# Layer 3's x on its way through DRAM: written in pieces of 128 bytes, read in runs of 512

## The chip, the cores and the metric

One Trainium2 chip, one of its cores. The metric is the device time of one launch of the whole kernel in microseconds (us). The kernel before takes 2758.63 us (median of three runs, 2754.33 to 2764.74).

## The reference

32 graphs of 512 nodes with 256 features, float32. Each graph goes through four layers, and after each its input is added and the sum is normalised over the features (layernorm):

```python
x = _layernorm(x + _L0_gnn_ref(x, adj, ...))        # relu(((1+eps) x + adj @ x) @ W1 + b1) @ W2 + b2
x = _layernorm(x + _L1_gnn_ref(x, adj, ...))        # attention of 4 heads over the edges, adj > 0.5
x = _layernorm(x + _L2_gnn_ref(x, adj, ...))        # attention of 8 heads, scores + log(adj)
x = _layernorm(x + _L3_gnn_ref(x, nodemask, adj, W))
```

The change is in layer 3, whose body is

```python
intermediate = jnp.einsum('bsh,hd->bsd', matrix, W)
similarities = jnp.einsum('bsd,btd->bst', intermediate, matrix) * adj
attn = softmax(where(mask, similarities, NEG_INF))
output = jnp.einsum('bst,bth->bsh', attn, matrix)
```

`matrix` is layer 3's x, 512 x 256. Both products that make the similarities need it with the features on the partitions; the last product and the residual need it with the nodes there.

## The kernel before

**Graphs and steps.** `graph(g)` describes the work of one graph as some 340 named steps, each with an engine, the steps it comes after and the buffers it takes. The graphs overlap: while one is in its layer 3, others are in their layers 0 to 2. The order in which all steps are issued is fixed by a text, `ORDER` (L40), which names for each place the next step. `Plan.run` (L180) reads it; an engine's queue gets its steps in that order. The due times that `Plan.run` adds up from the steps' written costs decide only which free slot of a kind a step takes (`room[kind].sort()`): `p` are the eight PSUM banks, `C` twelve SBUF tiles of about 4 KB per partition.

**Queues.** Plain DMAs are issued by SP, in order, and each waits in SP's queue for what it needs: adjacency (`la`, L806), x (`lx`, L818), layer 1's row factors to DRAM and back (`Rs`, `xs`, `Rl`, `hsb`, L1030 to L1054), the turn of x3 (`xw`, `xl`, L695 and L708) and the output (L1581). POOL issues accumulating copies from SBUF to SBUF, which add up layer 2's exponentials (L1311 and L1364), and the additions of biases to x (L610). Both kinds run on the same 16 DMA engines; the profile calls POOL's queue q0 and SP's q1.

**Layer 3's x.** The layernorm after layer 2 ends with four ScalarE steps `r30` to `r33` (L669), one for each chunk `c` of 128 nodes (`NC` = 4), which write the tile `x3`, [128 nodes, chunk, 256 + 1]. `x3` then has to be turned. The first two graphs and the last three do it on TensorE (`features_first`, L1214). The other 27, g = 2 to 28, call `turned(3, ...)` (L690):

- `xw3i`: one DMA writes all of `x3` to a DRAM tile, 1 KB a piece, after all four r steps;
- `xl30i` to `xl33i`: four DMAs read it back, block `a` of 32 features to the partitions 32a to 32a + 31, 32 values (128 bytes) a piece, into the tile `xL3`;
- `xe30`, `xe31`: two VectorE transposes of 32 x 32 blocks (L727) finish it to `xT3`, [128 features, half d, 512 nodes].

TensorE's steps `i0` and `i1` (iT_ps, L1504, issued by the helper at L327 or L331) are the first to read `xT3`. Behind the reads in SP's queue stand the adjacency loads of a later graph, then the output of the graph before and its x load.

Of the kernel before, what the change touches and what calls it, by code (L numbers as in the profile page):

```python
# [34 lines left out]
def row_bcast(ap, n):  # L35
# [2 lines left out]


ORDER = (  # L40
    'c-rk;*^=bA4Fo}ux~uw{@%D}<?En8tBNL#idcEV=h<$Q|)H78&cp-6+Dx@SLCAZiUY;jy-Po=2(Kg9|4bIQx=--7b0qlKcZttiWH'
    ')UVi3wM1o+(N!sO?!@kSboLOnRjaZznpU2Y$`ZAfigFx>7Bf_=cD7N9##YpPD_$7~C|;ijj(UEXt@>3xHy;76N3rVlOPui!^;)B1'
    'Ze~6<@4HqL?@k{BpjaHe4@7HgrzkZB5`)A)G;N7_%hThlvR`h%*6Krqs$-zO7j<HsYzpl{fE;>AQ!w0m*00uTE2l8Ejf-A4WNBW2'
    '4MJq#X=SuP5JH6P#V`c+U=X@h%2q=WQG{DGQ3DOr?6X2uJYkwxL1k7$g_Vt?mKP{STpw^dE>;>3pc5T!q^Ja=mN0cfntHDR6-}+u'
    'nAw>=j45i>kgBHehK2<CjV1-9U<=_7rvXvZ8qx+z1{47&mBZEmQM3)%hf9v}c)M=zYHS5n6Q(Fnd<EK~4WKa&-#CIwtMEFK7{TzX'
    'p3qbXlF&YFUbSH)=?-kNp&5Ewbe=<S%;9PD$dqkZcJ2{<3sX+_hDA^m<M{mmmU5a0J8Z25=0@P9VJi?by7t06RU56#iy5^PaRg;h'
    'GeisdYJgaVh$S>b^Rn|)sQh6(3}7(?$T2Kf#z<w1Q#sPg0Og(pQ>8j62%3Od8l5dHDV6+i$d+EAh<`A9wm6hRkpe&jO64G2EtP(m'
    '8wZM^hA*bYmNYelfl3SEfZ3RL=!KflI2=QV)Au8+0o1~8|MI?JI_#{mE5x-C)lzpxZ*3INOQj;!LqWQviyxIEmN7<I3E^4@;u>x2'
    'Apms=TZo7c_=f?`5N~X1_Ap<AUHEbHCdE#WT{zcZ4b8!=>OdFB16mA+P1B7c=qW8PK*+wrXd)`){F0y0Tn)<-j8dL-BaX8vBk?)X'
    'CwqScyl9Mr8G&B{CkxwpY9Q=Y($P*)O&Fu9o)Muw1+a6@ezs%I5*6@1$`2J}Oy_jY*q&pz)MR#_A^xcaD<kwjnn~xvF|R63B(@BA'  # L50
    'Et*Dv$TKo#K&%ah{umasoc;>gazXn`XrGrp7ql0&S3tO+y`a6Iy<+VJ?FH=x?FH=x?FH?%Lb$B<g7$*;3J90gUeI39UeNxZLp!kj'
    'HMGp+Cb&%9NVcJW6WqT5ZK5}zwXfLzDYW*C?K3b5?Z_CX=p)}0=x1&X*{&ya?a@kkK>J5zllPHXb9|M|f%@1@42GGYR^S(TJ3vFS'
    'gm8~3GbG1kWYM%_ww6WfnK&K?nMT$$D;PgB&zZx+2NL|k%zlaT7;5IPp=eS9*mDpO+y=6PNDx{b8F>lorRJHjEX;~psI!h_xIL1f'
    'gQ8)CLn6bCTw$U0F{_xMG$v6a4=p2A3pR*>J;Nk6c_oE=HT<A*uLOmlW^2r;m(xrNE%x-SikvO`X+fSa=44x<m}$*OWoPDnWV4xO'
    'rXsXiQ=Fp=8oUK*k>jt7JCAH<&;o)H!*0BKWwJha0>vJw?MUtNvjHm6u#@6_fn*`T<D?c<ij^a@;05SOABY`46+lJ?`jKNDJ3#>o'
    'PKBPFof`6!fiw&k))n-L<dk4|O53*6w>?bAA2<{aQh2q7hf6SSf-@seA>d?-aOlBG0HdM~Z8AWC6VQTt60wdH9VY6NlH-#_8<Ip^'
    'Am;<(P<^ct`zG)Y39VQQEjrTL+8{QyWTk*okz6E1Y{%LQSwO1^q&=Vm!9?rB2K7PQ3By8L4Ky4wLO}RoqCROCtq{<Y?qosAAR7!#'
    'wV2~X2UF%G1u5h6X-;x-r0O6nJZnbU7e$$zWFc?{nkHw)P8wE5^FT2e4uhBi{)1^N5mGdQEj<k^H8Rx7@K4Mo3S-U?fMK-MHd+cV'
    '0UwKiLAf=(_hIV1lA<P$WE4V#X~_VAbC*yeSa=L1G&CD?bV&|PP@956!Hr6$PeC~~nMKe>b_Tl0=?|t4buqq?l43Pt6y2*?ix@fh'
    'UKwUi?uhD;ffOnwQ6ktTUnW%yMbeGgIs*?md58~SuW(wSl8WUuGF=$qp2Ic2O0iUXFpzZUi@GP%NFO{Zx)zNo)<_z@NLh8nuMymz'  # L60
    'uEh*$BTxs551F5tWlt*#D>(`2=}S*cks!u>xsdbKFm<cJ71L0J=`)+kNV1DL?qs!CdD2H!J^3!DcQa5Eu0c1-s^mW9e3=;VVoV!='
    '`AdbgB28-GSi?OQEa&3o!E3TX9IJu%SoTGe^e;PEI-&T{^yu%Y_3?f7KPZ0BOQWykoLHXyA<F+^8~5(=^70~^TP9p7*|s|Zn)O*~'
    '@8ZrORF?0z`rE&HndhYceOAP=36slUrg_mH|Nen?dhat?wI-W4b^}?k%Cz~J*CNLuNp(D;twV0xA$3O(srYgLUdt{<2Gazls@Ya!'
    'vW1Mx!d1so%H}hPY#Ro`722|FvhJ_bzAww$y1z&;A>H#_ggN$SHYMfdwk*s1rjxX7*-P1dh|{rcL8xOG*j&728jMsfLH%kYfyydp'
    ')mZHYO_|MC&W5q$AIA~vWrucO?+&*^l6NTQ>ePPrzAQgcwEN-a=(<z)*|cl>&GkKdG@Yi-MiomgF5O&nb8MJiK_}ya4Ae0nS}ZFt'
    'FP+P`bJ^qyVo$z5&s}ZjI&-PLF+@#PkJ>qOTUU<p_WgUEFpGTKNG!!1KFNgU=G)|ooF>-+{`JWRR2s47^yU*b_9pvLxo~t1%v@b^'
    '{n3H}yK%A>TD(Wmvbg43=j>o_Z*N|`LxqlsnWHg7Fi?U8En>AN6PlW^xh(&5$aT^=S$vJ>g8}X>4kPw~c!AkPpZYvQVO?HQCz2#$'
    'u6k|XcO1Vm-mZ+Mj$t=DjwR&m(5AcfauZvyJ8t9-xA$rFzY36e!-nOe*Pco{?Gs(jK(o8<=t8~_C|v4cwc3IN9H4$m-rIbBVzy=g'
    '2mZmfZSE3SpZS6d8lIO79<Hp`K?s#L^nf)0mfV0mjM!FL*Y)PQSV5|Voh&Nv-fwp;AXH2atHWgR3*dqE4DX|2+qn9yk{s{V!Sb!F'
    ';_+Z!mQuI2NSR?%Q&yTnt{HbS7LkrX)_t$jw`n0+Uu>!#tUO{JsF1|w!~a|dO_s3lnFgL-K*b4%io?a~&95#uU~D%~V_oHRk`U*H'  # L70
    'avjmgg^o2gZd2S*`ebofVI6S;=;2+Gyd6&^+$+4$73CU{@B9&>!z>ZJaK8gd=MKuJx|_MuK2(B=84nV0sFVuUO5GP2iA(CrpCUXT'
    'htllOoCOH(0t5_ee2{<%PLRSK&ENf8`y@D@9#uTJdNZ5WwJzTCBKPlJ`gViv-``d49+Tad%iRY7QE{Vuw{}buZiv3?#`{p=ZMnL4'
    'nnzF#-YXwwU|?_ym~PXwo6+MuSSzAIU-=LO@6d&ebW9<LU_n)-1;TYabOASSy3e?iS-gn_igllGjN(337!Lz}cu{e?Yz{D%hP)SR'
    '?m`|H_*@0b-AbV2H5;d`gZ08l;)xBfyU`=#gBI>GWP3QEcBBjgq(7dvB0;3~X~buw`tc#+&J;Hxkk@N;rKaFBh(bT$b+>P~+wJY`'
    '<6eSY??L9Zn#Tr}m)=*d;2p<0VWQvPxon3MV@h#k{P4}AY2SPj<ZVj)h(QZ@&tK^|H^-2DCeiP6JW0{sq^<V!Bfie_QrpU(m2e-;'
    'Cq&%sSHgfPQR3$isxD$y87m6TsT%kHyva4P(@V@UK{ggSpUSCYVEn<uBT@;RF$Fvx*@<7AQiyO4+`Am{^PV4nljOjEb9<pG@HPLy'
    '-Nk<+D;KoCgqFz41?>gx6%a0HFK91luULCQdqI0adqI0adqI1x5H72|puM2I0>Wjr7ql0&7qtK9(DpA>i2n)g6S#mEp9^wQe-GTh'
    '0Ik>;Xv<e@{}ftz#`XzXTExUR&Zri7Y$vvoL|+BC@{H~iy!H(37i7;jL-A!jkLH84z}M)M;+Xzp168gvE$st)Asa%G+5<17%O3hf'
    '%S%~jauXYk!Nl?Y{deThe)BH*TC4gbNqblfa{H~y{mzu#3ymgT=*Bd?%oYNi$@d}wN)wP$!2bP^$krWYyyfa0rEK@Xztp5E3#hpX'
    '6o?K%q>BtTSTuf;>D+u7QYD`_Xvg3>v~{qBnL`8#HEs4J*h?@e08+e_4xAEVy6+JYHqubHBI|hbkOa@6%rDs9nNGL&U>oXjl(eMa'  # L80
    'eTv-tug;>&0=5ei#4U)=Ose1K*=7YZ0K=bYEH2rq(rLf27Law*^8#z|GD=%poBPC3Pe=swZB=1hw<^ccigsOkDIc9Lc$<ptYcY~F'
    'KuTUIC|_}8i{R)ETO;&+DNMHGMQ%*ZN-~#PyJZ^P5gOV>#<)<gk4FR|NzQj4(R7&Dr8<Kz4!R&x<rK1h_}`n<R}hSE#WA~)uzvSH'
    '2YlBXPV9~#e2Bn%ESvWZlAP#DmLJT4<i|2B75p4H*ZqEP%>julv&fNl{Gkps^4PB{2fnVff_)ialavc+cam24_9<9r$IHCdW!uO;'
    '0Oi9S0;Hy1U7sFs$gzb(gRN25btP%rCM%$xfb1Y`3ZfGg5(I^&GQ58T&%Via-vC#zp4=|hSJjyu6mR%AmSd5!%p)M9m+)NV*f*xt'
    '%c_!3I#kX(jGEH=gcom-D-}T{JdXjvzOb*7RK_<k+IVlIkWE8^+RvY)1_15PPY>>U-L}e5-TLZ-nA>FG=ZusxO+L(Cl*AzLF_Kv5'
    'k^R>CQJKt73ZKLi7<^`c4^R{hmXE?Qx3U&!ZY}woNLhmOF^l7HxIItW+5(GPmgduTBSRAtgind{TzW0tx~pyuhD&V>Fz5&LDh$k>'
    '!-Aq3!JI_n7TzPl*1>T32T(vNnl<<gGpVcR{5SgrGPGQBVi%|3c1xFDdRZsBm?)`y;WeOu)tFwve~1W29u&BDV9UCZHkik%3$FB+'
    '7gUf<Q92aq1^Ys_G1(Wve+JbSd>}Bpx_0o>R!7=BppkfMKjE&+E5!V#n^f!hdO|*>BQ;);sBm6Cmun-56#zIIyzHWOpP=142nB-P'
    'yo0!+ZG9=OC@(RinEL-|_Fy}$n6{>%+aSg*HoM(fom-no@z621y88HTOH#hwL){)o0G08!$__5&H=ifo`fKesyS;go_RWKcuOnu#'
    '(Aqk=*MK6{z<?*AjqgVkkRQR8fn*a2quqm&#}gT=7kT5fccT&bMZbEx?LLz2=6c)Q;|bHg3@;jSbMrH6UG!Yyb;OEkt}ZYpKOnkp'  # L90
    'n<FvLQ_NyhFb!iO^C-55W%=OJjy!B{TZ1>8kM@*!FC%%~Twl1vMnYRIRtjl!2l;sC(xP}1>cSVFvUZso$Wq<{`DA3)c^qqYKB*ed'
    'RB#@ZF;SgQu^J<aoNJ@=9kgSg4{Lm_^w<{i`Pi}B-h__gO@8qb+3-gB4`D>{SO'
)


# [122 lines left out]
def fast_path(  # L218
# [363 lines left out]
    def graph(g):  # L582
# [106 lines left out]

        def turned(n, more, src):  # L690

            @step(f"xw{n}i", "sp", 0.45, row(f"r{n}", NC))
            def _():
                t[f"xd{n}"] = dram.tile([P, NC, D], F32, tag=f"x{n}_dram", name=f"x{n}_dram_{g}")
                nc.sync.dma_start(t[f"xd{n}"], t[src][:, :, :D])  # L695

            transfer(f"xw{n}", 1.5, (f"xw{n}i",), land=6.0)

            for a in range(4):

                @step(
                    f"xl{n}{a}i", "sp", 0.66, (f"xl{n}{a-1}i",) if a else (f"xw{n}",),
                    take=() if a else (f"C=xL{n}/{2 if n == 1 else 1}",) + more,
                )
                def _(a=a):
                    if a == 0:
                        t[f"xL{n}"] = mid(f"xL{n}", [P, NC * DC, P], f"xL{n}")
                    nc.sync.dma_start(  # L708
                        t[f"xL{n}"][32 * a : 32 * a + 32].rearrange("j k (e i) -> j k e i", i=32),
                        bass.AP(  # L710
                            t[f"xd{n}"].tensor, t[f"xd{n}"].offset + 32 * a,
                            [[NC * D, 32], [P, NC * DC], [32 * NC * D, 4], [1, 32]],
                        ),
                    )

                transfer(f"xl{n}{a}", 1.0, (f"xl{n}{a}i",), land=6.0)

            for d in range(DC):

# [4 lines left out]
                def _(d=d):  # L724
                    if d == 0:
                        t[f"xT{n}"] = mid(f"xT{n}", [P, DC, N], f"xT{n}")
                    nc.vector.transpose(  # L727
                        t[f"xT{n}"][:, d, :].rearrange("p (c f) -> p c f", c=NC),
                        t[f"xL{n}"].rearrange("p (c d) f -> p d c f", d=DC)[:, d],
                    )  # L730

            plan.free(f"xL{n}", row(f"xe{n}", DC))
# [1349 lines left out]
```

## Time and profile before

| | |
|---|---|
| median of three runs | 2758.63 us |
| the profiled execution, its own time | 2757.91 us |
| its span, first to last instruction | 2756.2 us |
| PE / DVE / ACT / POOL busy | 98% / 78% / 62% / 17% |
| DMA engines: q0 (POOL) / q1 (SP) | 53.4% / 24.4% of 16 engines |
| writes of x3 to DRAM | 27 of 512 KB |
| reads back | 108 of 128 KB |
| mean granted TensorE clock | 0.992 |

Times are microseconds from the first instruction. PE is TensorE's matmuls, PEld its weight loads, DVE VectorE, ACT ScalarE, POOL GpSimd; a q behind the name is the engine's instruction queue, where waiting and the issuing of DMAs are seen. L708 is line 708 of the kernel. A group's name is written as output <- inputs by tile names without numbers, so `xL<-x_dram` is a read of the turn, `z<-z` an accumulating copy. A packet is one contiguous piece that a DMA engine moves.

### The profile page before, as it was taken

The numbers are of one execution on the slowest core, as the hardware profiler recorded it, in microseconds if no ns is written. First come the engines' busy times: TensorE is split into PE (matmuls) and PEld (weight loads), VectorE is DVE, ScalarE is ACT, GpSimd is POOL, SyncE is SP. The second block draws the span as 40 slices with busy tenths as digits, with TensorE's granted clock in tenths as the row PEclk, the third lists the DMA queues.
The fourth block names the chain that finished last, engine by engine and source line by source line (L and its number), as shares of the span: only waits on it lengthen the run. The fifth ranks groups of instructions, "written<-read, shape, count | busy, mean of one in ns | idle before, by whom it ended". The sixth has DMA issues, their size and how long they took to land.

```text
span 2756.2 us, 68553 instructions
## 1 busy us (share of the span) xinstructions
PE 2699.6 (98%) x28884; PEld 1309.0 (47%) x28884; DVE 2162.4 (78%) x4257; ACT 1716.5 (62%) x3320; POOL 480.4 (17%) x526
## 2 busy tenths in 40 slices
PE   8999999999999999999999999999999999898998
PEld 6534444444444444445444445454444454454443
DVE  3878778877878877879877879877878777477975
ACT  3666666666666666666666665666665665456854
POOL 1111121121111121111121111121111111111111
PEclk9999999999999999999999999999999999999999
DMA  8467797888888878888889878889787888756760
GB/s 169 81 137 148 162 164 163 170 158 162 168 155 152 173 161 162 159 158 154 169 161 170 155 154 158 176 159 170 147 160 149 175 154 159 153 93 150 152 127 33
DMA packets 476739, 418.80 MB, mean 152 GB/s; under 512 B 377789, under 2 KB 431497, under 8 KB 444553
## 3 DMA queue, kind: packets, MB, share of 16 engines
q0 software_dynamic: 45568, 277.89, 53.4%
q1 hardware_dynamic: 429872, 136.18, 24.4%
q8 instruction: 229, 3.75, 0.5%
q14 instruction: 86, 0.70, 0.1%
q10 hardware_dynamic: 984, 0.28, 0.1%
HBM read 155.53 MB, written 31.24 MB: 68 GB/s over the span
## 4 chain that ended last, share of the span: by engine, by line
PE 81%; DMA 4%; DVE 3%; issue 1%; ACT 1%; SPq 1%; POOL 0%; DVEq 0%; POOLq 0%; ACTq 0%
PE s L1278 8%; PE o_ps L1336 7%; PE o_ps L331 7%; PE o_ps L1122 6%; PE v_ps L331 6%; PE hT_ps L331 6%; PE y_ps L327 5%; PE h1T_ps L331 4%; PE s L331 4%; PE o2p_ps L331 4%; PE s L327 3%; PE iT_ps L327 3%; DMA z<-z 2%; PE qT_ps L327 2%; PE kT_ps L331 2%; PE kT_ps L327 2%
## 5 line engine op out<-in xcount | busy, mean ns | idle before, releaser
L1300 DVE SCALAR_TENSOR_TENSOR z<-AT,z 128x1024 f32<-128x1024 f32 x512 | 609.5, 1214 | 97.6 <-ACT z L1291 97.0
L1291 ACT ACTIVATE z<-s 128x512 f32<-128x512 f32 x1024 | 540.0, 607 | 141.3 <-PE s L1278 129.8
L1089 ACT ACTIVATE z<-R_bc,nT,S 128x512 f32<-128x512 f32 x512 | 374.6, 807 | 89.6 <-DMA z<-z 77.6
L669 ACT ACTIVATE x<-x,shift,rstd 128x256 f32<-128x256 f32 x508 | 273.8, 594 | 174.1 <-DVE shift L654 164.3
L1100 DVE SCALAR_TENSOR_TENSOR z<-z,T,edge 128x512 f32<-128x512 f32 x512 | 347.7, 744 | 16.5 <-ACT z L1089 16.4
L646 POOL TENSOR_TENSOR rstd<-ve,nhalf 128x4 f32<-128x4 f32 (+1 forms) x131 | 173.2, 1371 | 897.2 <-DVE ve L640 885.7
L1311 POOL DMA_DIRECT2D z<-z x186 | 174.8, 943 | 874.4 <-PE o_ps L1336 481.8
L1278 PE MATMUL s<-qT,kT 32*128 32x512 f32 x2048 | 272.8, 626 | 6.5 <-ACT kT L1249 6.5
L1336 PE MATMUL o_ps<-z,v 128*32 128x512 f32 x2048 | 249.7, 596 | 0.0
L1524 DVE TENSOR_TENSOR z<-s,AT 128x512 f32<-128x512 f32 x128 | 88.0, 690 | 204.1 <-PE s L327 104.0
L1150 DVE TENSOR_TENSOR z<-z 128x512 f32<-128x512 f32 (+1 forms) x256 | 229.5, 950 | 6.0 <-PE o_ps L1122 5.4
L1122 PE MATMUL o_ps<-z,v 128*32 128x512 f32 x2048 | 229.4, 593 | 1.1 <-ACT z L1291 1.1
L623 DVE BATCH_NORM_STATS2 st<-x 128x6 f32<-128x256 f32 x508 | 212.8, 419 | 11.0
L331 PE MATMUL o_ps<-x,z 128*32 128x257 f32 x3744 | 214.3, 380 | 0.0
L331 PE MATMUL hT_ps<-AT,x 128*32 128x384 f32 (+2 forms) x2592 | 181.5, 383 | 0.0
L327 PE MATMUL y_ps<-w_sb,h1T 128*128 128x256 f32 x816 | 180.9, 379 | 0.0
L1278 PEld LDWEIGHTS s<-qT,kT 32*128 32x128 f32 x2048 | 96.6, 184 | 142.0 <-issue 52.8
L331 PEld LDWEIGHTS o_ps<-x,z 128*32 128x32 f32 x3744 | 120.9, 110 | 87.8 <-issue 5.7
L327 PEld LDWEIGHTS y_ps<-w_sb,h1T 128*128 128x128 f32 x816 | 152.9, 190 | 19.6
L331 PE MATMUL h1T_ps<-hT,w_sb 128*32 128x512 f32 x1312 | 147.2, 592 | 0.0
L610 POOL DMA_DIRECT2D x<-biases x96 | 107.2, 1139 | 177.5 <-issue 72.5
L1122 PEld LDWEIGHTS o_ps<-z,v 128*32 128x32 f32 x2048 | 65.3, 110 | 149.3 <-issue 125.3
(188 smaller groups left out, 3913.1 us busy)
## 6 DMA issues: line engine op xcount, KB each, us to landing
z<-z POOLq DMA_DIRECT2D x186, 1024.0 KB, 8.8
x<-biases POOLq DMA_DIRECT2D x96, 512.0 KB, 10.0
R_bc<-R_dram SPq DMA_DIRECT2D x32, 1024.0 KB
Ar<-in_adj_dram SPq DMA_DIRECT2D x124, 256.0 KB
z<-z POOLq DMA_DIRECT2D x62, 512.0 KB, 7.5
x<-in_x_dram SPq DMA_DIRECT2D x32, 512.0 KB
out_dram<-x SPq DMA_DIRECT2D x31, 512.0 KB
x_dram<-x SPq DMA_DIRECT2D x27, 512.0 KB
```

The source lines that it names most:

```text
L327: nc.tensor.matmul(out, lhsT, rhs, start=start, stop=stop)
L331: nc.tensor.matmul(out[part], lhsT[:, part], rhs, start=start, stop=stop)
L623: nc.vector.bn_stats(t[f"st{n}"][:, c, :], t["xo" if n == 4 else "x"][:, c, :D])
L669: nc.scalar.activation(t[into][:, c, :D] if into else xn, xn, AF.Identity, bias=t[f"shift{n}"][:, c : c + 1], scale=t[f"rstd{n}"][:, c : c ...
L1089: nc.scalar.activation(t[f"e{h}"][:, c, :], t["Rbc"][:, h, :], AF.Relu, bias=t["nT"][:, h, c : c + 1], scale=t["S"][:, h, c : c + 1],)
L1100: nc.vector.scalar_tensor_tensor(z, z, t["T"][:, h, c : c + 1], t["edge"][:, c, :], op0=ALU.add, op1=ALU.mult)
L1122: nc.tensor.matmul(po[32 * q : 32 * q + 32, :], t["v"][:, c, hp * P + 32 * q : hp * P + 32 * q + 32], t[f"e{2*hp+q//2}"][:, c, :], start=( ...
L1150: nc.vector.tensor_add(z[:, :m, :], z[:, :m, :], z[:, m : 2 * m, :])
L1278: nc.tensor.matmul(pk, t["k"][hs, o, blk(c)], t["q"][hs, o, :], start=True, stop=True)
L1291: nc.scalar.activation(t[f"E{k}"][:, j, :], t[f"ps{k}{j}"], AF.Exp, scale=QSCALE)
L1300: nc.vector.scalar_tensor_tensor(z, t["AT"][:, c, None, :].to_broadcast([P, 2, N]), ADJ_EPS, z, op0=ALU.add, op1=ALU.mult,)
L1336: nc.tensor.matmul(t[f"n{o}"][32 * j : 32 * j + 32, :], t["v2"][:, c, o * P + F2 * j : o * P + F2 * (j + 1)], t[f"E{k}"][:, j, :], start=( ...
```

## The change

The DRAM tile gets another layout, [128 nodes, 8 blocks of 32 features, chunk, 32] for [128 nodes, chunk, 256]. The write becomes four DMAs, one for each chunk, each after its own r step; a piece is 32 features, 128 bytes, and lands 512 bytes from the next. The four reads then find the 32 features of the four chunks side by side: 128 values, 512 bytes a piece. `xL3` holds them in another order, so the transposes read it through a pattern of more dimensions; what they write is the same. `ORDER` is rewritten so that the steps of all engines keep their sequence, with the new write steps where the old one stood. The written costs of the transfer's steps change too; they bear on the choice of slots.

```diff
@@ -38,58 +38,58 @@
 ORDER = (
-    ...
+    ...
 )
@@ -689,31 +689,37 @@
 
         def turned(n, more, src):
 
-            @step(f"xw{n}i", "sp", 0.45, row(f"r{n}", NC))
-            def _():
-                t[f"xd{n}"] = dram.tile([P, NC, D], F32, tag=f"x{n}_dram", name=f"x{n}_dram_{g}")
-                nc.sync.dma_start(t[f"xd{n}"], t[src][:, :, :D])
-
-            transfer(f"xw{n}", 1.5, (f"xw{n}i",), land=6.0)
+            for c in range(NC):
+
+                @step(f"xw{n}{c}i", "sp", 0.5, (f"r{n}{c}",))
+                def _(c=c):
+                    if f"xd{n}" not in t:
+                        t[f"xd{n}"] = dram.tile([P, DC * 4, NC, 32], F32, tag=f"x{n}_dram", name=f"x{n}_dram_{g}")
+                    nc.sync.dma_start(
+                        t[f"xd{n}"][:, :, c],
+                        t[src][:, c, :D].rearrange("p (k i) -> p k i", i=32),
+                    )
+
+                transfer(f"xw{n}{c}", 1.0, (f"xw{n}{c}i",), land=1.3)
 
             for a in range(4):
 
                 @step(
-                    f"xl{n}{a}i", "sp", 0.66, (f"xl{n}{a-1}i",) if a else (f"xw{n}",),
+                    f"xl{n}{a}i", "sp", 0.45, (f"xl{n}{a-1}i",) if a else row(f"xw{n}", NC),
                     take=() if a else (f"C=xL{n}/{2 if n == 1 else 1}",) + more,
                 )
                 def _(a=a):
                     if a == 0:
-                        t[f"xL{n}"] = mid(f"xL{n}", [P, NC * DC, P], f"xL{n}")
+                        t[f"xL{n}"] = mid(f"xL{n}", [P, DC, NC * P], f"xL{n}")
                     nc.sync.dma_start(
-                        t[f"xL{n}"][32 * a : 32 * a + 32].rearrange("j k (e i) -> j k e i", i=32),
+                        t[f"xL{n}"][32 * a : 32 * a + 32].rearrange("j d (e i) -> j d e i", e=4),
                         bass.AP(
-                            t[f"xd{n}"].tensor, t[f"xd{n}"].offset + 32 * a,
-                            [[NC * D, 32], [P, NC * DC], [32 * NC * D, 4], [1, 32]],
+                            t[f"xd{n}"].tensor, t[f"xd{n}"].offset + a * NC * 32,
+                            [[NC * D, 32], [4 * NC * 32, DC], [32 * NC * D, 4], [1, NC * 32]],
                         ),
                     )
 
-                transfer(f"xl{n}{a}", 1.0, (f"xl{n}{a}i",), land=6.0)
+                transfer(f"xl{n}{a}", 0.4, (f"xl{n}{a}i",), land=0.9)
 
             for d in range(DC):
 
@@ -725,8 +731,8 @@
                     if d == 0:
                         t[f"xT{n}"] = mid(f"xT{n}", [P, DC, N], f"xT{n}")
                     nc.vector.transpose(
-                        t[f"xT{n}"][:, d, :].rearrange("p (c f) -> p c f", c=NC),
-                        t[f"xL{n}"].rearrange("p (c d) f -> p d c f", d=DC)[:, d],
+                        t[f"xT{n}"][:, d, :].rearrange("p (c e i) -> p c e i", c=NC, e=4),
+                        t[f"xL{n}"][:, d].rearrange("p (e c i) -> p c e i", e=4, c=NC),
                     )
 
             plan.free(f"xL{n}", row(f"xe{n}", DC))
```

## The prediction

> **What bounds the kernel now.** I read the page first, then the chain in order of time, PE's and DVE's waits, and the timelines of SP, DVE and PE around one turn of x3. Graphs are numbered g = 0 to 31 as in the code; the turn by DMA is made for g = 2 to 28, 27 graphs.
>
> ```profile
> span 2756.2 us, 68553 instructions
> PE 2699.6 (98%) x28884; PEld 1309.0 (47%) x28884; DVE 2162.4 (78%) x4257; ACT 1716.5 (62%) x3320; POOL 480.4 (17%) x526
> q0 software_dynamic: 45568, 277.89, 53.4%
> q1 hardware_dynamic: 429872, 136.18, 24.4%
> ```
>
> TensorE is busy 98% of the span. The DMA engines are busy 78%, two thirds of it with POOL's accumulating copies (q0). In the chain, the same matmuls return at a fixed distance, 82.96 us:
>
> ```profile
> 629.81 6.91 PE y_ps L327 x32
> 712.77 6.91 PE y_ps L327 x32
> 795.73 6.91 PE y_ps L327 x32
> ```
>
> So from about 550 to 2100 us TensorE sets the pace alone, and a change of transfers can win nothing there; it can only lose, by making TensorE wait. What can be won stands among the waits:
>
> ```profile
> PE iT_ps L327 <- DVE xT L727: 13.3, 2, 12.9
> DVE xT L727 <- DMA xL<-x_dram: 20.8, 4, 15.0
> ```
>
> Both lines are this transfer. PE's 13.3 us are two waits: 0.38 us at 2293 (g = 25) and 12.93 us at 2370 (g = 26). In the timeline of a steady graph (g = 10) the turn looks like this (start, duration, engine, line):
>
> ```profile
> 1027.93 0.58 SPq L695 DMA_DIRECT2D x_dram<-x  x1
> 1036.23 7.22 SPq L708 DMA_DIRECT2D xL<-x_dram  x4
> 1043.63 6.63 SPq L806 DMA_DIRECT2D Ar<-in_adj_dram  x4
> ```
>
> and the transposes that need it, in DVE's timeline, followed by PE's first matmul on them:
>
> ```profile
> 1049.84 1.30 DVE L727 STREAM_TRANSPOSE xT<-xL 128x512 f32<-128x512 f32 x2
> ...
> 1051.37 1.88 PE L327 MATMUL iT_ps<-xT,w_sb 128*128 128x512 f32 x4
> ```
>
> The write takes 8.3 us until the reads may be issued, and the last read lands at 1046.9 by its semaphore: 3.0 us before DVE comes to the transpose, which follows its own queue without idle time. Over the steady graphs this slack is 0.1 to 3.3 us (least 0.12 at g = 13, where xL landed 20.1 us and DVE came 20.2 us after the write's issue). TensorE's second matmul, the first to need the second transpose, has 0.65 us more (1051.80 against 1051.15). That slack is what the change spends or adds to.
>
> **How the transfer shares the DMA engines.** By the trace's packet records, while q0 has a backlog each engine takes one q1 packet for one q0 packet, whatever its size: at 1198 to 1201 us 23 to 25 q1 packets beside 23 to 24 of q0 per us. In quiet, q1 runs 1200 packets of 128 B per us (13 ns each on 16 engines). So a transfer that meets a burst of q0 practically ends when the burst ends, plus its remaining packets at the quiet rate.
>
> **The change part by part.**
> *The order.* Decoded with the kernel's own reader, PE, ACT, DVE and POOL keep their 2077, 3193, 3242 and 509 steps in the same sequence. SP has 548 for 467 steps: three more writes per turned graph, directly ahead of the old one. Buffers are the same up to g = 23; in g = 24 to 31 493 choices of banks and slots differ. Those have no row; waits of PE after 2190 us other than this transfer's are 5.92 us and several of about 1 us, so I take 0 with ends of -6 and +6 us.
>
> *The write.* 512 packets of 1 KB (mean 49.5 ns) become 4096 of 128 B. No row shows a 128 B write to DRAM. Below it stands the 128 B read of the same tensor, 13 ns; above it the 512 B writes of R_dram and xs_dram, 34.8 ns, and further up the 1 KB write, 49.5 ns. At 1 KB direction costs nothing (median 46 ns for x_dram<-x and for x<-in_x_dram), so I take the read of equal size, 13 ns. Three quarters of it start earlier: the ACT steps r30 to r33 end 2.7, 2.2, 1.0 and 0.03 us before today's issue, and in that stretch q0 is quiet in the steady graphs. SP sits idle from 1003.3 to 1027.9 in g = 10, so three more issues of 0.6 to 0.75 us cost nothing; if SP were busy they would put off the reads by as much. The new waits on single rows have only this graph's writes and reads queued behind them.
>
> *The read.* 4096 packets of 128 B become 1024 of 512 B: at 34.8 ns 2.2 us on 16 engines where now 3.7 us pass from the first packet to the last in quiet graphs. With a quarter of the pieces the third issue no longer blocks SP (up to 7.3 us today); the adjacency loads behind it start no later, and their transposes (L865) waited only 6.2 us in all.
>
> *Sum for a steady graph, g = 12* (one unbroken burst; times from today's issue, 1193.56): quiet from -1.4 (first issue -2.65 plus the 1.24 us to a first packet in quiet) to +0.15, 1.55 x 1230 = 1900 pieces; 219 during the burst, as many as 1 KB packets passed; 1977 left at +12.0, 1.6 us; landing 0.45: +14.1, against +14.3 now. Reads: 1.36 to the first packet, 2.2, landing 0.9: +18.6, against +21.3 now and +22.2 where DVE needs it. The slack grows by 2.7 us, nothing else moves: 0 us. Graphs with a gap in the burst (g = 10) come out alike if 1500 to 1800 pieces fit the gap of 1.5 us, and if not, the +14 case holds, still 3 us early.
>
> *Ends, g = 25 and 26.* At g = 25 the reads land some 2 us sooner: -0.4 us. At g = 26:
>
> ```profile
> 2348.82 0.56 SPq L695 DMA_DIRECT2D x_dram<-x  x1
> 2361.57 10.67 SPq L708 DMA_DIRECT2D xL<-x_dram  x4
> ...
> 2372.28 4.54 SPq L806 DMA_DIRECT2D Ar<-in_adj_dram  x1
> ```
>
> ```profile
> 2382.96 3.78 PE L327 MATMUL iT_ps<-xT,w_sb 128*128 128x512 f32 x4 [12.93 <-DVE xT L727]
> ```
>
> ```profile
> 2370.00:2383.00 13.00, 0.07 (x2) 0.04 (x1) 0.81 (x2) 2.73 (x5) 1.79 (x3) 0.63 1.24 191
> 2383.00:2398.00 15.00, 15.00 (x112) 5.58 (x116) 4.14 (x9) 6.07 (x13) 0.00 (x0) 0.86 0.78 199
> ```
>
> (windows: PE, PEld, DVE, ACT, POOL, clock, DMA, GB/s). After the stall the clock is halved until 2387.1: 4.1 us at half speed, 2.1 us lost. Here the rows of x3 end within 1.5 us and q0 is busy from 2347.9, with gaps only at 2358.4 to 2360.4, 2369.2 to 2370.5 and from 2378.3. Writes: 2460 pieces in the first gap and about 250 beside the bursts; the last 1400 need the second gap (which passed 1946 packets of 128 B now). The reads then wait for the third: 2378.3 + 2.2 + 0.9 = 2381.4, against 2382.1 now: -0.7 us.
>
> *The transposes.* DVE reads xL in steps of 128 values, 32 at a time; L727 takes 668 to 712 ns, L1431 with its stepped input 698: no change, ends 0 and +0.05 us each, under the 0.65 us above.
>
> *DMA load.* 512 x 49.5 + 4096 x 17 (mean of all 128 B packets) = 95 us of engine time per graph becomes 4096 x 17 + 1024 x 34.8 = 105 us, of some 1035 (78% of 16 x 83): POOL's copies hardly notice.
>
> *Total.* -0.4 - 0.7 = -1.1 us against the profiled execution's own 2757.9 us; the median of the three runs is 0.7 above it: 2757.5 us.
>
> [...]
>
> **The rivals.**
> *Slower: the small writes are dear.* Place: the write, behind q0's burst, in each of some 24 steady graphs. At a price p per piece (rate R = 16/p) the reads land at 12.0 + (3877/R - 1.55) + 4.9; with the 0.65 us TensorE starts to wait from +22.85, that is p = 31 ns, in the tightest graph (+20.85) from 23 ns. At 34.8 ns it is +23.8: 1 us each, up to 3 in the tight ones, 24 x 1.2 = 29 us: 2787. At 49.5 ns +27.4: 4.5 x 24 = 108 us, before any halving of the clock: 2866. For it: the nearest writes are above 31 ns. Against: equal prices of both directions at 1 KB.
> *Slower in the tail only.* At g = 26 the writes miss the second gap, the reads follow 5 to 8 us later and the halved clock lasts longer, or new buffers add a wait: +5 to +14, 2766. For it: 1400 pieces against a gap of 1.3 us leave little.
> *Faster.* The whole wait goes: 12.9 + 0.4 + 2.1 = 15.4 us: 2743. For it: it is the largest stall in the trace. Against: writes and reads would both have to be through by 2370.5, and 4096 pieces do not fit the first gap; bursts would have to shift.
>
> **How the numbers follow.** Forecast 0.53 (own range 2752 to 2764: run spread and -6 to +6 of the tail); faster 0.14; dear writes 0.22; tail 0.11, of which 0.04 over the bound. What a measurement can tell from no change is about 0.5%, 13.8 us. Faster 0.14, same 0.53 + 0.07 = 0.60, slower 0.26. Range 2742 to 2790: takes in the faster case and writes up to 34.8 ns; about 0.06 below and 0.11 above are left out.
>
> **What would show it.** Right: y_ps still 82.96 us apart; L727 without idle time on DVE in steady graphs; SP's reads issued in under 2 us together; xL landing 2 to 3 us sooner; 128 B packets of writes near 13 ns; PE's wait at 2370 near 12 us. Wrong: a PE wait on xT in each graph with a clock below 1.00 (dear writes), a changed period, or the 2370 wait gone.

## The result and the profile after

The changed kernel takes 2763.3 us (median of 12 runs, 2760.8 to 2769.0), the kernel before beside it 2760.5 us (12 runs, 2754.3 to 2766.5): a ratio of 1.0018, 95% interval 1.0010 to 1.0027. Measured once more it was 2760.4 against 2759.4 us, ratio 1.0006 (0.9997 to 1.0015). By these two ratios the change costs some 2 to 5 us in 2760, and the second cannot be told from nothing; I forecast a gain of 1.1. The result lies inside the bound of 0.5% that I took for "same", but the sign of the sum was wrong, and this section and the next look for the terms that were.

The page of the changed kernel, its head and the two queues that matter:

```profile
span 2762.7 us, 68704 instructions
...
PE 2702.8 (98%) x28884; PEld 1309.7 (47%) x28884; DVE 2163.1 (78%) x4257; ACT 1715.2 (62%) x3320; POOL 479.6 (17%) x526
...
q0 software_dynamic: 45568, 277.89, 53.4%
q1 hardware_dynamic: 444992, 136.18, 23.8%
```

q1 carries 15 thousand packets more and is busy for less of the time (24.4% before): by the packet records the 128 B write took 12.3 to 14.1 ns a packet (means by graph; median 13), and the 512 B read 27 to 28 ns in quiet, 38 to 43 where it met other traffic.

TensorE's pace, in the chain that ended last (start, duration):

```profile
634.10 6.91 PE y_ps L327 x32
...
717.08 6.91 PE y_ps L327 x32
...
800.09 7.17 PE y_ps L327 x32
```

The distance is 82.98 and 83.01 us, 82.96 to 82.98 in most graphs. The waits by what ended them (total us, times, longest):

```profile
DVE xT L733 <- DMA xL<-x_dram: 23.2, 4, 16.4
...
PE iT_ps L327 <- DVE xT L733: 15.1, 3, 14.3
```

Against 20.8 us and 13.3 us before: the transfer is waited for longer. A steady graph, g = 10, on SP's queue:

```profile
1029.73 7.94 SPq L698 DMA_DIRECT2D x_dram<-x  x4
1047.97 2.84 SPq L714 DMA_DIRECT2D xL<-x_dram  x4
1050.99 5.48 SPq L812 DMA_DIRECT2D Ar<-in_adj_dram  x4
```

The first of the four writes is issued at 1029.73, 2.6 us ahead of the end of the last row chunk (`r33`, 1032.37). The last one is held until 1037.67, and the reads come at 1047.97, 15.6 us after `r33`; in the profile before they came 8.3 us after it. DVE's transpose of the same graph:

```profile
1054.52 1.30 DVE L733 STREAM_TRANSPOSE xT<-xL 128x512 f32<-128x512 f32 x2
```

It still follows DVE's own queue without a wait, but the last read landed at 1053.26 us, 1.3 us ahead of it, where it had been 3.0. And the tail, g = 26 (SP; then TensorE; then windows with the busy times, the granted clock and the DMA share):

```profile
2352.13 13.53 SPq L698 DMA_DIRECT2D x_dram<-x  x4
2376.59 5.51 SPq L714 DMA_DIRECT2D xL<-x_dram  x4
2382.14 0.85 SPq L812 DMA_DIRECT2D Ar<-in_adj_dram  x1
```

```profile
2389.14 3.78 PE L327 MATMUL iT_ps<-xT,w_sb 128*128 128x512 f32 x4 [14.32 <-DVE xT L733]
```

```profile
2375.00:2389.00 14.00, 0.00 (x0) 0.00 (x0) 0.62 (x1) 2.58 (x5) 2.77 (x5) 0.59 1.12 180
2389.00:2404.00 15.00, 14.86 (x96) 5.33 (x100) 3.50 (x7) 5.42 (x11) 0.00 (x0) 0.82 0.91 212
```

The wait grew from 12.93 to 14.32 us, and the clock, granted at 0.50 from 2377.5 us on, is back at 1.00 at 2394.5 us, 5.4 us after TensorE resumed, instead of 4.1.

Where do the 6.5 us between the two profiled executions lie? From the starts of the y_ps groups, graph by graph: +0.5 us up to 461 us, +3.8 between 461 and 551 us, +0.9 over the steady part (551 to 2045 us), +2.0 around the wait of g = 26, -0.7 elsewhere. The 3.8 us have nothing to do with `xT` on their face: TensorE waited 3.15 us for `R_t`, 1.08 before, behind an adjacency load, and its clock was granted at 0.50 for 3.41 us behind that wait (503.55 to 506.97 us), where it was 1.00 before.

### The profile page after: what moved, and what is told of

It reads as the page before. It is cut to its first block, busy times and chain, and to the rows that moved or that the text cites. A ratio compares the mean times of both kernels' runs of the same rounds, so it can differ in the third digit from the quotient of the medians.

```text
span 2762.7 us, 68704 instructions
## 1 busy us (share of the span) xinstructions
PE 2702.8 (98%) x28884; PEld 1309.7 (47%) x28884; DVE 2163.1 (78%) x4257; ACT 1715.2 (62%) x3320; POOL 479.6 (17%) x526
## 4 chain that ended last, share of the span: by engine, by line
PE 80%; DMA 6%; DVE 3%; ACT 1%; issue 1%; SPq 0%; POOL 0%; DVEq 0%; POOLq 0%; ACTq 0%
PE s L1284 8%; PE o_ps L1342 7%; PE o_ps L331 6%; PE o_ps L1128 6%; PE v_ps L331 6%; PE hT_ps L331 6%; PE y_ps L327 5%; PE s L331 4%; PE h1T_ps L331 4%; PE o2p_ps L331 3%; PE iT_ps L327 3%; PE s L327 3%; DMA z<-z 3%; PE qT_ps L327 2%; PE kT_ps L331 2%; PE kT_ps L327 2%
## 5 line engine op out<-in xcount | busy, mean ns | idle before, releaser
L327 PEld LDWEIGHTS y_ps<-w_sb,h1T 128*128 128x128 f32 x816 | 152.8, 190 | 19.9 <-DVE y L1201 0.3
```

The lines of the kernel that those rows point to most:

```text
L327: nc.tensor.matmul(out, lhsT, rhs, start=start, stop=stop)
```

## The experiments

All kernels but the unaltered ones and the two with g = 26 on TensorE have the buffers of the kernel before, given by a table; the order of the steps is that of the changed kernel, or, where a graph turns x3 as before, that of before. Times from here on are counted from the end of `r33` where a sign stands before them.

### The changed kernel again (c_after, c_after2)

> The changed kernel once more, unaltered. If its added 2.8 to 5 us belong to the change, the median lies 2 to 6 us above the kernel before on the same chip, with a wait of about 14 us for x3's transpose near 2375 us and a y_ps period of 82.98 us. The rival is one profile's accident: the wait for R_t near 500 us (3.15 us, with 3.4 us of half clock behind it, 1.08 us before) made 3.8 of the 6.5 us between the two profiles; by this rival it falls back to about 1 us and the span to about 2759 us.

> The changed kernel unaltered, for a third profile: the wait near 2370 us at 14.3 us again, the wait for R_t near 500 us either about 1 or 3.2 to 3.5 us; if it is 1 us, the time is about 2759 us, else about 2765 us.

c_after: 2760.4 us (2758.7 to 2767.0), the ratio 1.0006 given above, so 1 to 2 us above the kernel before, at the low end of what I expected or below it. The profiled execution took 2765.7 us, the second longest of the 11, with 14.31 us of waiting for `xT` in g = 26 and 3.50 us for `R_t`. c_after2: 2763.7 us, 14.28 us and 1.30 us. The wait of g = 26 is a property of the kernel. That for `R_t` is not fixed, and the guess that it settles between 2759 and 2765 us was wrong: with 1.30 us the time was still 2763.7. In both profiles TensorE also waits 1.37 us just before 400 us ("near 398 us" in the texts below), for `xT` of g = 2, which was in neither profile compared so far.

### The kernel before again (c_before)

> The kernel before once more, for a second profile. The four profiles with early or small writes all show a wait of 3.2 to 3.5 us for R_t near 500 us, where the one profile of before shows 1.08. If that wait is a matter of how q0 and q1 happen to meet in one execution, this profile shows it at about 3.4 us too, or another value between 0 and 4; if it belongs to the changed writes, it shows 1.0 to 1.2 us again.

2763.4 us, span 2761.7. The chain of waits of the two profiles of the same kernel, first the one that the prediction was made from, then this one:

```profile
473.32 19.64 DMA Ar<-in_adj_dram
```

```profile
473.23 22.53 DMA Ar<-in_adj_dram
```

```profile
503.75 0.28 PE L1020 MATMUL R_t<-ident,R 128*18 128x128 f32 x1 [3.96 <-ACT R L1003]
```

Two executions of one program differ by 5.5 us of span, 4.4 of them here: a load that starts at the same time takes 2.9 us more (by the packet records it is left with q0's packets beside it until 495 us in the second, where q0 paused near 489 us in the first), TensorE waits 3.96 us for `R_t` instead of 1.08, and the matmuls behind the wait run slower: 2.42 us for the four of `qT_ps` and 1.96 for the sixteen of `d_ps`, 1.88 and 1.09 in the first. So the largest part of the difference between the first two profiles is no proof of anything.

### Buffers as before (c_slots)

```diff
-                free, i = room[kind].pop(0)
+                i = given[g, key]
+                free = next(f for f, j in room[kind] if j == i)
+                room[kind].remove((free, i))
```

> The change with the buffers and banks of the kernel before in all graphs (493 choices put back by a table), the same order of steps. If the other buffers in g = 24 to 31 cause the loss, the time falls to that of the kernel before within 1 us and the wait near 2370 us to 12.9 us. If the loss comes from how the pieces travel, the time stays within 1 us of the changed kernel and the wait stays at 14 us.

2763.3 us, ratio 1.0012 (1.0004 to 1.0021), wait in g = 26 14.31 us. The 493 other choices of buffers are not the cause.

### The two halves of the change (e_layout, e_chunk)

e_layout has the new layout and waits for all four rows with the first write; e_chunk has the four early writes in the old layout, in pieces of 1 KB, and the old reads:

```diff
-                @step(f"xw{n}{c}i", "sp", 0.5, (f"r{n}{c}",))
+            @step(f"xw{n}i", "sp", 0.5, row(f"r{n}", NC))
...
+                for c in reversed(range(NC)):
                     nc.sync.dma_start(
                         t[f"xd{n}"][:, :, c],
```

```diff
-                nc.sync.dma_start(t[f"xd{n}"], t[src][:, :, :D])
+                    nc.sync.dma_start(t[f"xd{n}"][:, c, :], t[src][:, c, :D])
```

> The layout alone: pieces of 128 bytes and reads of 512 bytes, but no write starts before the last row chunk is done (four writes issued behind one another, buffers as before). By my theory (the end of the write misses the quiet stretch of q0 and goes one piece for one packet of q0) all 4096 pieces now start 2.6 us later: the write lands at +15 to +17 us in graphs with an unbroken burst, the reads at +20 to +22, the wait near 2370 us grows to 15 to 20 us, and the time lies 2 to 12 us above the changed kernel. By the rival (it is the early, separate issues that cost, by holding SP) the time equals that of the kernel before within 2 us.

> The early start alone: four writes by row chunk in the old layout (pieces of 1 KB) and the old reads in runs of 128 bytes, buffers as before. By my theory only 128 packets are left when the last row chunk is done, at 24 packets per us beside a burst 5.3 us: the write lands at +6 to +8 us, the 4096 pieces of the reads then run beside the burst and end 3 to 4 us after it, at +16 to +18 (before +21); the steady period is 82.96 us, the wait near 2370 us 8 to 13 us, the time 0 to 6 us below the kernel before. By the rival (separate early issues cost) it lies 2 to 5 us above.

e_layout: 2769.4 us, ratio 1.0037 (1.0023 to 1.0052). e_chunk: 2761.8 us, ratio 1.0007 (0.9999 to 1.0016). The means over the 16 steady graphs g = 8 to 23, in us from the end of `r33`, from SP's issues, the completions of the DMAs and DVE's transposes:

| kernel | last write lands | first read issued | last read lands | DVE comes | least slack of a graph | TensorE waits, sum |
|---|---|---|---|---|---|---|
| before | +8.7 | +9.1 | +19.8 | +21.8 | 0.12 | 0 |
| before, c_before | +9.6 | +10.0 | +20.0 | +22.2 | 0.68 | 0 |
| after | +13.3 | +13.6 | +20.3 | +21.8 | 0.02 | 0.2 |
| after, c_after | +13.9 | +14.3 | +20.3 | +22.1 | 0.02 | 0.95 |
| after, c_after2 | +12.3 | +12.9 | +19.9 | +22.0 | 0.38 | 0 |
| e_layout | +17.0 | +17.0 | +22.2 | +22.6 | 0.02 | 5.2 |
| e_chunk | +4.1 | +5.7 | +18.5 | +21.9 | 0.12 | 0 |
| e_quiet (below) | +6.2 | +6.4 | +11.5 | +22.4 | 8.8 | 0 |

This table is the heart of the case. The two halves work against each other. Starting early brings the write forward, by 4.6 to 5.5 us in the old layout (from +8.7 or +9.6 to +4.1) and by 3.1 to 4.7 in the new one (+17.0 to +12.3 to +13.9). The small pieces put it back by 8 to 10 us at equal starts (+4.1 against +12.3 to +13.9). From issue to landing the reads then take 3 to 4.6 us less (10.0 and 10.6 us before, 6.0 to 7.0 after). Only a part of that is the longer reads: of the reads issued after +13, behind the burst, the old ones of 128 B took 6.4 to 6.5 us (means of the two profiles of the kernel before), the new ones 5.1 to 5.2. The longer read is worth some 1.3 us; the rest is that the late reads no longer meet the burst. Together the last read lands where it did before, within 0.5 us.

e_chunk on SP's queue in g = 10, to be laid beside the lines of the changed kernel:

```profile
1028.54 2.99 SPq L733 DMA_DIRECT2D x_dram<-x  x4
1036.85 9.29 SPq L746 DMA_DIRECT2D xL<-x_dram  x4
1046.32 6.10 SPq L844 DMA_DIRECT2D Ar<-in_adj_dram  x4
```

Pieces of 1 KB: no issue is held up, and the reads follow 5.7 us after `r33` instead of 15.6. In 12 graphs it is no longer the write that the reads wait for: they wait, up to 3.9 us, for TensorE's `o_ps` (L1160).

Of my numbers for these two, the wait in g = 26 was wrong both times: 13.6 us in e_layout (15 to 20 expected), 13.2 in e_chunk (8 to 13 expected) although its write there landed 10 us sooner than the changed kernel's (+12.7 against +22.9). The reason stands in the section on the prediction. And e_chunk did not gain the 0 to 6 us that I expected: it came out level with the kernel before or some 2 us above it (-0.3 to 4.4 us by the interval), so that the time alone does not refute the rival of that text. The slack that it won in the steady graphs is time for which nothing waits, and its profile has 2.02 us of waiting in g = 25 (0.38 and 0.41 before) and 3.37 us for `R_t`.

### q0 without its bursts (e_quiet)

```diff
-                src, dst = (t[f"E{b}"].rearrange("p h n -> p (h n)") for b in (k, a))
+                src, dst = (t[f"E{b}"].rearrange("p h n -> p (h n)")[:, :64] for b in (k, a))
...
-                    nc.gpsimd.dma_start(z[dst], z[src], accum_op=ALU.add)
+                    nc.gpsimd.dma_start(z[dst, :64], z[src, :64], accum_op=ALU.add)
```

> The changed kernel with POOL's accumulating copies of the second layer cut from 2048 to 64 values per row, so that q0's packets there shrink from 8 KB to 256 bytes; 31 of 32 sums of the attention's denominators are left out. If q0's bursts hold the small pieces back (one piece for one packet), the last write now lands 2 to 3 us after the last row chunk (13 to 14 us with the bursts), the last read 7 to 9 us after it, no graph waits for xT, and the time falls by 15 us or more. By the rival (the pieces themselves, or the issues on SP, are slow) the write still lands 8 us or more after the last row chunk.

2717.7 us, ratio 0.9843 (0.9825 to 0.9861). No graph waits for `xT`; the last write lands at +6.2, the last read at +11.5 (last row of the table). Both are later than I expected; one burst stayed, the copies of the biases, 4 KB rows, which in g = 10 fall into the write for some 3 us. The full bursts delay the write by 6 to 8 us more than that (+12.3 to +13.9 in the changed kernel). The 42 us are more than x3's part, since other waits on these copies go too.

### Which graphs lose (e_mid, e_head, e_tail, e_only2, e_no2)

Each makes the change in some graphs only:

```diff
+            early = 8 <= g <= 24      # e_head: g < 8; e_tail: g >= 25; e_only2: g == 2; e_no2: g > 2
+            if early:
```

> The change in g = 8 to 24 alone, where TensorE sets a steady pace; all other graphs turn x3 as before, buffers as before. If the steady graphs carry the loss (the slack of xL shrank from 2.05 us on average to 1.5 to 1.8, and single graphs wait 0.1 to 0.8 us), these waits add up to 0.2 to 1.5 us here, and the head (wait for R_t near 500 us) and the tail (wait near 2370 us) stand as before, 12.9 us in the tail: the time lies within 1.5 us above the kernel before. By the rival, a cost in every graph (queue time, DMA load), the y_ps period is above 82.97 us in most graphs and the time is 2 to 5 us above.

> The change in g = 25 to 28 alone, buffers as before. With the steady graphs worth 0 (the run with g = 8 to 24 alone had a ratio of 1.000), the loss must sit in the head or in the tail. If in the tail: the wait near 2370 us is 14.3 us instead of 12.9 to 13.1, the halved clock behind it as long or 3.4 us longer, and the time lies 1 to 3 us above the kernel before. By the rival (the head) the ratio is 1.000.

> The change in g = 2 to 7 alone, buffers as before. If the head carries a part, the wait for R_t near 500 us is 3 us or more in more of its executions than before (there it was 0.6, 0.7, 1.1 and 4.0 us in four profiles), and the time lies 1 to 3 us above the kernel before. By the rival (the tail alone) the ratio is 1.000 and this wait may take any value.

> The change in g = 2 alone, buffers as before. If this graph makes the loss of the head, TensorE waits 1.1 to 1.4 us near 398 us (0 before), the last read lands at 396.5 us or later behind the burst, and the time lies 1 to 3 us above the kernel before. By the rival (the loss comes from g = 3 to 7, or the wait for R_t falls by chance) the ratio is 1.000.

> The change in all graphs but g = 2, buffers as before. If g = 2 makes the loss of the head, no wait stands near 398 us, the wait for R_t near 500 us is above 3 us no more often than before, and only the tail's part is left: the wait near 2370 us at 14.3 us, the time 0 to 2 us above the kernel before. By the rival the time stays 2 to 4 us above and R_t waits 3 us or more.

| changed graphs | median us | ratio (95%) | wait near 398 us | wait for R_t near 500 us | wait in g = 26 |
|---|---|---|---|---|---|
| none (before; c_before) | | | 0; 0 | 1.08; 3.96 | 12.93; 13.05 |
| 8 to 24 (e_mid) | 2759.5 | 1.0000 (0.9989 to 1.0010) | 0 | 0.69 | 13.35 |
| 25 to 28 (e_tail) | 2759.2 | 1.0007 (0.9998 to 1.0016) | 0 | 0.36 | 14.32 |
| 2 to 7 (e_head) | 2759.9 | 1.0012 (1.0001 to 1.0023) | 1.29 | 3.42 | 13.21 |
| 2 (e_only2) | 2760.9 | 1.0002 (0.9993 to 1.0011) | 1.44 | 3.34 | 13.63 |
| 3 to 28 (e_no2) | 2761.0 | 1.0005 (0.9996 to 1.0014) | 0 | 0.99 | 14.30 |

The times alone separate little. The steady graphs come out at nothing, and only the head's ratio has an interval that leaves out 1; the three parts add up to 1.0019 and the two of the split at g = 2 to 1.0007, where the whole change showed 1.0018, 1.0006 and, in c_slots, 1.0012. The waits say more, though each profile is one execution (that of e_only2, 2764.7 us, was the second longest of its 11). The wait of g = 26 is 14.3 us in all profiles of the table, and in those of the unaltered changed kernel, in which g = 26 is changed, and 12.9 to 13.6 in all in which it is not. The wait near 398 us appears only where g = 2 is changed: 1.1 to 1.4 us in six of the eight profiles with the new layout in that graph (e_quiet aside), none in the first profile of the changed kernel and in e_pe26_new (below). Here is why, on SP's queue, before and with g = 2 alone changed (e_only2):

```profile
364.19 16.87 SPq L806 DMA_DIRECT2D Ar<-in_adj_dram  x3
381.17 1.19 SPq L695 DMA_DIRECT2D x_dram<-x  x1
385.75 3.18 SPq L708 DMA_DIRECT2D xL<-x_dram  x4
```

```profile
364.70 16.87 SPq L883 DMA_DIRECT2D Ar<-in_adj_dram  x3
381.68 3.82 SPq L736 DMA_DIRECT2D x_dram<-x  x4
389.47 4.94 SPq L752 DMA_DIRECT2D xL<-x_dram  x4
```

```profile
400.00 3.64 PE L366 MATMUL iT_ps<-xT,w_sb 128*32 128x512 f32 x32 [1.44 <-DVE xT L799]
```

SP is not idle here: it is held by an adjacency load until 381 us, long after `r33` (370 us). Nothing can start early, and four issues take 3.8 us where one took 1.2. The reads come 3.7 us later, at 389.47 instead of 385.75, and that is just at the start of a burst of q0: before, some 3000 of the 4096 pieces had passed by then, by the packet records, and now none has. DVE's transpose comes at 399.1 us (392 to 396.5 in the profiles with g = 2 unchanged), and TensorE waits. In the two profiles without the wait the reads were issued earlier, at 387.0 and 385.4 us.

It is the small pieces that make the reads late, not the three more issues. e_chunk has four issues in g = 2 too, of pieces of 1 KB:

```profile
380.38 2.68 SPq L733 DMA_DIRECT2D x_dram<-x  x4
385.05 3.33 SPq L746 DMA_DIRECT2D xL<-x_dram  x4
```

From the first write's issue to the first read's it takes 4.7 us there, 4.6 in the kernel before, and 6.5 to 7.9 in the eight profiles with the new layout; e_chunk has no wait here.

The wait for `R_t` was 3.15 us or more in 8 of the 9 profiles in which g = 2 has early writes, small writes or both (e_quiet aside) and in 1 of the 6 without (e_no2's 0.99 and e_only2's 3.34 are the closest pair). That the shift of g = 2 brings the adjacency load of g = 6 into a worse meeting with q0 more often would fit this, but I have only the count for it, and two profiles speak against it: in e_chunk the reads of g = 2 land no later than before (395.6 against 396.3 us), and `R_t` waits 3.37 us; in c_after2 they land late (399.0), and it waits 1.30. With c_before at 3.96 the long wait needs no change at all. Its cause stays open.

### What the wait in g = 26 is worth (e_pe26, e_pe26_new)

```diff
-        near = g < 2 or g >= B - 3
+        near = g < 2 or g >= B - 3 or g == B - 6
```

The order has, for g = 26, two transposes of TensorE behind layer 1's two of g = 28, and ACT's two copies behind theirs, in place of the DMAs and DVE's transposes.

> The kernel before, but in g = 26, the only graph with a long wait for the turn by DMA, x3 is transposed by TensorE and copied out by ACT as in the last three graphs. If this one wait and the halved clock behind it are all that the turn costs, the time falls by 10 to 17 us, to 2742 to 2750 us, with 0.9 us more work of TensorE. By the rival (another wait stands right behind it: DVE, ACT or a load) most of the 12.9 us appears elsewhere and the time falls by less than 5 us.

> The changed kernel with x3 of g = 26 transposed by TensorE, buffers as in the run of the kernel before with the same edit, which took 2744.2 us (ratio 0.9937). If the wait in g = 26 is where the change loses, both agree within 1 us. If the head or the steady graphs carry the loss, this one is 2 to 4 us slower, at 2746 to 2748 us.

e_pe26: 2744.2 us (2740.6 to 2746.6), ratio 0.9937 (0.9923 to 0.9951), the fastest kernel of this study that computes the whole result, and 15.5 us below the kernel before. The two transposes that replace the transfer, and the matmul that waited 12.93 us, in TensorE's timeline, and the windows:

```profile
2362.53 1.04 PE L1224 MATMUL xT_t<-ident,x 128*128 128x128 f32 x8
...
2370.50 1.88 PE L325 MATMUL h1T_ps<-hT,w_sb 128*128 128x512 f32 x4
2372.22 3.60 PE L325 MATMUL iT_ps<-xT,w_sb 128*128 128x512 f32 x8
```

```profile
2370.00:2385.00 15.00, 15.00 (x115) 5.54 (x117) 3.60 (x7) 8.56 (x17) 2.92 (x5) 1.00 0.99 188
2385.00:2400.00 15.00, 15.00 (x276) 8.39 (x272) 14.16 (x29) 11.23 (x17) 0.00 (x0) 1.00 0.39 107
```

No idle time, clock 1.00: nothing stood behind this wait. The same edit on the changed kernel (e_pe26_new) gives 2746.1 us (2743.4 to 2751.4), ratio 0.9963 (0.9950 to 0.9976): 2 us above e_pe26 by the medians, and beside its own runs of the kernel before it gains 12.0 us where e_pe26 gains 15.5, though the two intervals touch. So 2 to 4 us of the change's cost seem left without g = 26. Its profile has the wait for `R_t` at 3.26 us, e_pe26's at 0.62, and no wait near 398 us in either; that this is where the rest lies is likely and not shown.

## Why the prediction was wrong

**Right: what bounds the kernel.** TensorE's pace did not move (82.98 us; e_mid 1.0000), the transposes cost the same (692 ns a piece against 691), the buffers cost nothing (c_slots), and the forecast of "no change that a measurement of 0.5% can tell" held. That the steady graphs came out at nothing, as forecast, was luck as far as the sum goes: the slack was not spent, but the sum that said so was wrong, as the third point shows.

**Right: the price of a small write.** I took 13 ns for a write of 128 B from the read of that size, and it measured 13 (median). The rival of the dear writes, 2787 us, falls. In bytes a small piece does move less in the same time: 128 B in 13 ns are 9.8 bytes per ns of an engine, 512 B in 28 ns 18.

**Wrong: the steady sum.** "The slack grows by 2.7 us" rested on g = 12. There the old write landed at +14.3, so that 4096 pieces at +14.1 lost nothing. (Its first row ended 3.1 us ahead of the issue; the 2.7 that I used are those of g = 10.) But g = 12 has the latest old write of all steady graphs: the mean is +8.7, and only 5 of the 16 graphs g = 8 to 23 lie above +13. In the others, 512 packets of 1 KB slip into a gap of q0 that 4096 pieces do not fit (in g = 10, 510 of them between 1031 and 1034 us); of the changed kernel's writes 13 of 16 lie above +13. The head start was smaller, too: of the 1900 pieces that were to have passed by +0.15, 1000 to 2000 had, about 1000 in 7 of the 16 graphs, where the second issue was held for 1.3 to 2.0 us.

I saw the case and let it pass, with "if 1500 to 1800 pieces fit the gap of 1.5 us, and if not, the +14 case holds, still 3 us early". In g = 10 the gap near 1036 us passed some 1000 pieces, 995 and 778 followed at 1045 and 1046 us, and the reads came at +15.6. Of the two ends that I named, the second was the rule, and "3 us early" was false as well: reads were priced at 4.5 us from issue to landing, and in quiet they take 5.0 to 5.3 us: SP spends 0.6 us on each of the four issues (2.84 us together in g = 10; I had asked for less than 2), and the 1024 packets pass at 240 to 350 per us there, not at the 460 that 34.8 ns would allow. The expected gain of 2.7 us became a loss of 0 to 0.5 us on average. This cost next to no time, since some 2 us of slack were there (e_mid 1.0000).

**Wrong: nothing for g = 2.** The sum was worked out for a steady graph, where three quarters of the write start ahead of `r33`, and the graphs of the head got the same 0 us without a row of their own. In g = 2 SP is held until 10 us after `r33`, so that no piece starts early, and 4096 of them then need 2 to 3 us more than 512 of 1 KB; the reads meet the burst, and TensorE waits 1.1 to 1.4 us in six of eight profiles. I had named the condition ("if SP were busy they would put off the reads by as much") and did not look for a graph that meets it. But the price that I put on it, the three more issues, was not what came: by e_chunk they cost nothing even there. What does hold SP is the writes themselves: in the first profile of the changed kernel the seven write issues that began with 2048 pieces not yet moved, by the packet records, took 3.2 to 9.0 us (4.2 in g = 10, 9.0 for the third write of g = 26), the other 101 at most 2.4. The longest of these 101, the fourth of g = 26, began with some 2700 pieces left, as a gap of q0 opened.

**Wrong: g = 26, -0.7 us.** The frame held: 2660 pieces passed in the first gap (2460 expected), the rest in the second, the reads in the third. But the wait grew, to 14.3 us from 12.9 to 13.6, for two reasons that the packet records show. The third gap opened 30.9 us after `r33` and not 29.4, as the burst ahead of it lasted about a microsecond longer (why, I did not find), and the 1024 packets of the reads, at up to 440 per us, needed 3.8 us from the opening to the landing where I had 3.1. e_chunk shows the other side: a write that is through at +12.7 leaves 4096 pieces of reads, which end in the same third gap, at +33.6. With either layout one side of the transfer has 4096 pieces and the reads end in the third gap. The rival "slower in the tail only" was right about the place and about little else: the writes did not miss the second gap, the new buffers added no wait (c_slots), and the wait grew by some 1.3 us for its +5 to +14.

**Wrong: g = 25, -0.4 us.** The wait there was 0.61, 0.34 and 1.76 us in three profiles of the changed kernel, 0.38 and 0.41 before: no gain.

**The sum.** -1.1 us was forecast. What the profiles show is some +1.3 us of wait in g = 26 where the sum had -0.7 (the clock there, granted at 0.50 for 13.65 us in the first profile of the kernel before and for 17.07 us in that of the changed one, is not counted), 0 to +1.4 in g = 25 where it had -0.4, 1.1 to 1.4 in g = 2 in most profiles and 0 to 1 in the steady graphs where it had 0, and more often than not 2 to 3 us behind the wait for `R_t`. The last of these is only a count, and its cause is open. The first four turn the sign; how much each is worth in the median is below what these runs can tell.

**The rival "faster".** Its price was right: 15.4 us for the whole wait, and e_pe26, which takes away that of g = 26, recovered 15.5 us (13.5 to 21 by its interval). That this change would not reach it was also right.

## What to carry to other kernels

In these traces a transfer that shares the DMA engines with large packets of another queue gets one packet in for each of theirs, at 128 B as at 1 KB (in a us, 24 or 25 of 128 B beside 23 to 25 of 8 KB in g = 10 of the changed kernel, 22 to 25 of 1 KB beside 23 or 24 of 8 KB in g = 12 before): what counts there is the number of its pieces, and a layout that makes the reads four times longer by making the writes eight times more numerous only moves the jam. Work a sum out for the typical graph and not for the one whose timeline is at hand: a table of landings over all graphs of the profile before would have shown that g = 12 was the exception. And where one wait of 13 us is all that a transfer costs, take that one instance off the transfer, as e_pe26 does: 1.0 us of TensorE's time for a wait of 12.9.

## What the runs showed of the hardware

- Beside a burst, q1 and q0 alternate packet by packet: 24, 25 and 24 pieces of 128 B beside 24, 25 and 23 packets of 8 KB in the three us from 1038 us on (g = 10).
- A write of 128 B to DRAM costs an engine as little as a read (13 ns), so a small piece is cheap in quiet, and in a burst one goes by for each packet of 8 KB, which takes an engine about 0.67 us, an estimate from 24 packets per us on 16 engines (median of the packet records 0.64).
- Reads of 512 B in quiet passed at 240, 267 and 350 packets per us in g = 10, after four issues 0.6 to 1.0 us apart; at 28 ns a packet 16 engines would pass some 570. That the issues are the limit is likely and was not tested.
- One program's wait for the same load was 1.08 us in one execution and 3.96 in another, with the load starting at the same time to 0.1 us. A difference of 5 us between two single profiles of this kernel needs a second profile of each.
